# L3_xattn's queries by halves of two token tiles, one batch each, in a perceiver kernel on Trainium2

## The chip, the cores and the metric

The kernel runs on one core of a Trainium2 chip. A core has TensorE (PE, matrix products; the loading of its stationary operand is a row of its own, PEld), VectorE (DVE), ScalarE (ACT), GpSimd (POOL) and SyncE (SP), which issues the DMAs. Each engine works through its own queue in order and waits on semaphores of the others. The metric is the device time of one launch in microseconds; a figure for a kernel is the median of its runs. Lines of a profile name a line of the kernel's source (L702), an engine, an operation and the tiles it writes and reads.

## The reference: what is computed

The program is a perceiver of four layers. x holds 2 batches of 256 latent tokens with 256 features, the context 2 batches of 4096 tokens. Each layer adds a cross-attention to the context, a self-attention and a feed-forward block to x. The change touches only the cross-attention of the last layer, L3_xattn, and in it only the way of the queries:

```python
def _focus(x, focusing_factor):
    x = jnp.abs(jnp.where(x >= 0, x, LEAKY_SLOPE * x)) + EPS
    nrm = x.mean(axis=-1, keepdims=True)
    return jax.nn.softmax(jnp.log(x) * focusing_factor, axis=-1) * nrm
...
q = _focus(q @ Wq.T, focusing_factor)
k = _focus(k @ Wk.T, focusing_factor)
qh, kh, vh = (_to_heads(q), _to_heads(k), _to_heads(v))
qh = _topk_sparsify(qh)      # of each head's 16 features the 11 largest stay, the rest become 0
kh = _topk_sparsify(kh)
k_mean = kh.mean(axis=1)
z_inv = jnp.einsum('bnd,bd->bn', qh, k_mean) + EPS
kv = jnp.einsum('bnc,bnd->bcd', kh / sqrt_l, vh / sqrt_l)
y = jnp.einsum('bnc,bcd->bnd', qh, kv) / z_inv[..., None]
...
return y @ Wp.T
```

Here n is the 256 latent tokens for the queries, and x is layer-normalized ahead of the block.

## The kernel before

The 512 latent tokens (T) of both batches stand as four tiles of 128 tokens (NT = 4), two to a batch. x is kept with features on the partitions, as two chunks of 128 features. The blocks run one after the other. The context's keys for L3 are sharpened, ranked and summed much earlier, in the shadow of the cross-attentions of layers 0 and 1 (class `Focus`, called from the two attentions' step loop); these use `Focus.weigh` with four tiles and `Focus.sparsify`, which ranks on VectorE. L3_xattn itself (`l3_xattn`) has only the queries left:

1. `net.center` and `net.measure` take the mean off x and find each token's reciprocal deviation (`rstd`). The kept sums of keys (`focus.kc`) are turned and multiplied by `wv` to one small matrix for each batch (`kv_ps`, then the tiles `kv`).
2. For each token tile TensorE multiplies x by `wq` into a quarter of `q_ps`, a PSUM tile of two banks. `Focus.magnitudes` (L620, L621) reads it twice on ScalarE, as the positive and the scaled negative part, each with its sum over features, and POOL adds the two parts.
3. `Focus.weigh` takes the logarithm of all four tiles in one ScalarE instruction (L628), the product with the focusing factor on POOL (L632), the negative maximum of each token on VectorE (L634) and one exponential for each tile on ScalarE (L637). [...]
4. `sparsify_by_products` finds each feature's rank in its head. POOL scales the result (L687). The features are laid out so that feature e of all eight heads of a chunk stand side by side; then 15 comparisons on VectorE (`ge`, L699), shifted by 1 to 15 features, cover all pairs. Each is added to and taken from the rank by products with the identity (L702) and its negative (L703), which accumulate in PSUM. A comparison covers all four tiles; the rank has two banks with two tiles each, so each comparison is followed by four products. At the end VectorE keeps what has a rank below 11 (L706), one instruction for each bank, into `kept`.
5. Then, tile by tile, TensorE turns `kept` (`from_tokens`, L582, copied out by L219 as `qT`), multiplies it by the batch's matrix (`lin_ps`), VectorE forms the reciprocal and the quotient `y` (L1916 to L1920), TensorE turns `y` and a copy brings it to `yT`. `add_projection` multiplies by `wp` and adds x.

PSUM has three kinds of buffers here: two `mm` banks (also those of `from_tokens`), two `sc` tiles of two banks each (`q_ps` and `rank`) and two `acc` banks (`lin_ps`). The order of the instructions in each engine's queue in this block is not written by hand: the framework's scheduler arranges the instructions from their order in the program and from its own estimates. The next block, L3_attn, begins with POOL fills of its tiles, which wait until the tiles of L3_xattn are free.

Of the kernel before, what the change touches and what calls it, by code (L numbers as in the profile page):

```python
# [19 lines left out]
F32 = mybir.dt.float32  # L20
BF16 = mybir.dt.bfloat16
I32 = mybir.dt.int32
AF = mybir.ActivationFunctionType
ALU = mybir.AluOpType
AX = mybir.AxisListType

P = 128
NB = 2
S = 256
# [564 lines left out]
class Focus:  # L594
# [28 lines left out]
    def weigh(self, y, total, factor):  # L623


        nc = self.nc
        top, norm = (self.net.sm(NT, name=n, tag=n) for n in ("f_top", "f_norm"))
# [8 lines left out]
        for t in range(NT):  # L636
            nc.scalar.activation(  # L637
                y[:, t, :], y[:, t, :], AF.Exp, bias=top[:, t : t + 1], accum_out=norm[:, t : t + 1]
            )
            if t % 2:  # L640
                yield
# [39 lines left out]
    def sparsify_by_products(self, pool, out, y, factor):  # L681

        nc, net = self.nc, self.net
        N8, G = NT * ND, H // ND
        w = y.rearrange("p t (m e) -> p (t m) e", m=ND)
        for t in range(NT):
            nc.gpsimd.tensor_scalar(out[:, t, :], y[:, t, :], factor[:, t : t + 1], 1.0, ALU.mult, ALU.mult)  # L687
        minus = pool.tile([P, P], BF16, name="minus", tag="minus", bufs=1)
        nc.vector.tensor_scalar_mul(minus, net.ident16, -1.0)
        rank = net.sc("rank").rearrange("p i (h e) -> p i h e", e=P)  # L690
        half = N8 // 2
        for i in range(2):
            nc.tensor.matmul(
                rank[:, i], lhsT=net.ident16, rhs=self.rank0.unsqueeze(1).to_broadcast([P, half, P]), start=True, stop=False
            )
        for s in range(1, DH):
            n = (DH - s) * G
            ge = pool.tile([P, N8, P], BF16, tag="ge", name="ge", bufs=3)
            nc.vector.tensor_tensor(ge[:, :, :n], w[:, :, :n], w[:, :, P - n :], ALU.is_ge)  # L699
            for i in range(2):  # L700
                of = ge[:, i * half : (i + 1) * half, :n]
                nc.tensor.matmul(rank[:, i, :, P - n :], lhsT=net.ident16, rhs=of, start=False, stop=False)  # L702
                nc.tensor.matmul(rank[:, i, :, :n], lhsT=minus, rhs=of, start=False, stop=s == DH - 1)  # L703
        flat = out.rearrange("p t d -> p (t d)").rearrange("p (i h e) -> p i h e", i=2, e=P)
        for i in range(2):
            nc.vector.scalar_tensor_tensor(flat[:, i], rank[:, i], float(KEEP), flat[:, i], ALU.is_lt, ALU.mult)  # L706
# [1156 lines left out]
def l3_xattn(net, x):  # L1863
# [4 lines left out]
    with tc.tile_pool(name="l3x", bufs=1, reuse_waits="tile") as big, tc.tile_pool(name="l3x_w", bufs=2, reuse_waits="tile") as work:  # L1868
# [27 lines left out]
        total = net.sm(2, NT, name="f_total", tag="f_total")  # L1896
        q_ps = net.sc("q_ps").rearrange("p i (t d) -> p (i t) d", d=D)
        for t in range(NT):
            at = slice(t * P, (t + 1) * P)
            net.matmuls(q_ps[:, t, :], [(c[:, at], wq[:, d, :]) for d, c in enumerate(norm.chunks)])  # L1900
            focus.magnitudes(work, q, total, t, q_ps[:, t, :], (norm.rstd[:, t : t + 1], low[:, t : t + 1]))
        factor = net.sm(NT, name="f_factor", tag="f_factor")
        run(focus.weigh(q, total, factor))
        kept = big.tile([P, NT, D], F32, name="kept", tag="kept")
        focus.sparsify_by_products(work, kept, q, factor)
        yT = big.tile([P, ND, T], F32, name="yT", tag="yT")
        G = H // ND
        for t in range(NT):
            at, b = slice(t * P, (t + 1) * P), t * P // S
            qT = work.tile([P, ND, P], F32, name="qT", tag="qT")  # L1910
            net.from_tokens(lambda m, k: qT[:, m : m + k, :], kept[:, t, :], ND)
            ps = net.acc("lin_ps")[:, : ND * (P + G)].rearrange("p (m e) -> p m e", m=ND)
            for m in range(ND):
                net.matmuls(ps[:, m, :], [(qT[:, m, :], weigh[b, m])])
            r = net.sm(ND, G, name="r")
            nc.vector.tensor_scalar_add(r, ps[:, :, P:], 1e-6)  # L1916
            nc.vector.reciprocal(r, r)
            y = work.tile([P, D], F32, name="y", tag="y")
            for m in range(ND):
# [408 lines left out]
```

## Time and profile before

| what | value |
|---|---|
| median of 3 runs | 2512.33 us |
| lowest and highest run | 2512.18 and 2951.45 us |
| the profiled execution's own time | 2515.34 us |
| its span, first to last instruction | 2513.4 us |
| mean granted TensorE clock in it | 0.958 |
| first `low` of L3_xattn's queries (L620) starts at | 2098.93 us |
| first comparison (L699) starts at | 2114.53 us |
| first transpose of `kept` (L582) starts at | 2125.83 us |
| projection of L3_xattn starts at | 2140.07 us |

Times within the profile are counted from the start of the span. The granted clock is a share of TensorE's full speed. A line of the timeline gives start, length, engine, source line, operation, result and operands with their shapes, how many instructions were merged, and in square brackets how long the engine was idle before and who ended that. The length of an instruction contains its own run-through time, so two neighbours on an engine can overlap in such lines.

### The profile page before, as it was taken

What the parts mean: (1) busy time and instruction counts of PE and PEld (TensorE: products, weight loads), DVE (VectorE), ACT (ScalarE), POOL (GpSimd) and SP (SyncE); (2) the same over time, 40 slices, a digit from 0 to 9 for tenths busy, and PEclk for the clock granted to TensorE, in tenths of its full rate; (3) what the DMA queues carried; (4) which work ended last, traced back from release to release, by engine and by line L of the source; (5) the groups of instructions that cost most, each with busy time, mean ns of one, the idle gap of its engine ahead of it and who ended that gap; (6) DMA issues with size and microseconds to landing.
All of it is one profiled execution on the core that took longest, in us unless ns stands there. A gap on an engine that the chain in (4) does not pass through costs nothing.

```text
span 2513.4 us, 42846 instructions
## 1 busy us (share of the span) xinstructions
PE 2336.0 (93%) x17142; PEld 1252.9 (50%) x17142; DVE 1549.4 (62%) x2719; ACT 1093.2 (43%) x1917; POOL 333.2 (13%) x505
## 2 busy tenths in 40 slices
PE   7999999999999689999999999989999996889998
PEld 3455455544544364554454544554448453455454
DVE  4878888788736757877878778443241354334343
ACT  2456555555615333555555565531131252123232
POOL 3000001000024602000010000000011031002120
PEclk9999999999989799999999999989999997798989
DMA  5432232132010133322222220201232100100100
GB/s 185 138 105 86 88 96 94 52 111 64 10 38 35 48 103 108 101 91 90 90 94 86 77 98 28 83 14 43 96 100 93 43 18 14 34 21 12 58 12 21
DMA packets 97798, 174.42 MB, mean 69 GB/s; under 512 B 15120, under 2 KB 63888, under 8 KB 96704
## 3 DMA queue, kind: packets, MB, share of 16 engines
q1 hardware_dynamic: 97600, 171.68, 21.1%
q8 instruction: 136, 2.23, 0.4%
q14 instruction: 62, 0.51, 0.1%
HBM read 154.25 MB, written 0.59 MB: 62 GB/s over the span
## 4 chain that ended last, share of the span: by engine, by line
PE 57%; DVE 6%; ACT 2%; issue 1%; POOL 0%; DMA 0%; SPq 0%; ACTq 0%; DVEq 0%; POOLq 0%
PE s L1113 6%; PE s L1137 5%; PE proj L180 5%; PE attn_acc L1161 5%; PE v_ps L180 4%; PE expert L180 2%; PE k_ps L1034 2%; PE s L180 2%; PE c_acc L1753 2%; PE s L1430 2%; PE ffn_ps L180 2%; DVE mx L1121 2%; PE scores L342 1%; PE f_ps L180 1%; PE kc_sum L180 1%; PE qk_ps L180 1%
## 5 line engine op out<-in xcount | busy, mean ns | idle before, releaser
L1121 DVE TENSOR_REDUCE mx<-s 128x2 f32<-128x1024 f32 x512 | 603.2, 1221 | 224.6 <-PE s L1113 221.8
L1147 ACT ACTIVATE p<-s 128x1024 f32<-128x1024 f32 x512 | 496.0, 1021 | 255.8 <-PE s L1137 253.8
L1137 PE MATMUL s<-xa_q,xa_k 32*128 32x256 f32 x4096 | 342.3, 403 | 26.0 <-DVE mx L1121 23.0
L1113 PE MATMUL s<-xa_k,xa_q 32*128 32x512 f32 x2048 | 338.7, 642 | 7.0 <-ACT p L1147 2.3
L1137 PEld LDWEIGHTS s<-xa_q,xa_k 32*128 32x128 f32 x4096 | 212.7, 184 | 167.5 <-issue 92.6
L1161 PE MATMUL attn_acc<-p,xv 128*32 128x256 f32 x4096 | 276.2, 386 | 0.7 <-ACT p L1147 0.7
L1113 PEld LDWEIGHTS s<-xa_k,xa_q 32*128 32x128 f32 x2048 | 111.4, 183 | 124.7 <-issue 60.6
L667 DVE TENSOR_TENSOR ge<-fy 128x960 bf16<-128x960 f32 (+14 forms) x240 | 169.5, 706 | 6.5
L1161 PEld LDWEIGHTS attn_acc<-p,xv 128*32 128x32 f32 x4096 | 107.4, 109 | 131.4 <-issue 84.4
L621 POOL TENSOR_TENSOR fy<-fy,low 128x256 f32<-128x256 f32 x64 | 46.4, 725 | 881.3 <-ACT fy L620 881.1
L669 DVE TENSOR_TENSOR rank<-rank,ge 128x960 bf16<-128x960 bf16 (+14 forms) x240 | 104.2, 434 | 6.0
L671 DVE TENSOR_TENSOR rank<-rank,ge 128x960 bf16<-128x960 bf16 (+14 forms) x240 | 100.8, 420 | 2.6
L387 POOL TENSOR_SCALAR p<-p,r 128x128 f32<-128x128 f32 (+1 forms) x192 | 82.6, 442 | 127.0 <-DVE r L383 72.4
L1081 ACT COPY xv<-v_ps 128x512 f32<-128x512 f32 x64 | 37.6, 587 | 135.7 <-PE v_ps L180 135.7
L368 ACT ACTIVATE p<-p,top 128x256 f32<-128x256 f32 (+1 forms) x128 | 57.1, 447 | 66.6 <-DVE top L356 65.3
L180 PE MATMUL f_ps<-f_wk,f_ctx 128*128 128x256 f32 x256 | 68.9, 400 | 0.6 <-DMA f_ctx<-in_ctxT 0.6
L1034 PE MATMUL k_ps<-ctx_k,w_L0x_wq 128*64 128x512 f32 x256 | 66.0, 612 | 3.2 <-DMA ctx_k<-in_ctxT 2.9
L180 PE MATMUL v_ps<-w_L0x_wv,ctx_v 128*128 128x256 f32 x256 | 65.6, 400 | 0.8 <-ACT k_dense L1047 0.8
L180 PEld LDWEIGHTS f_ps<-f_wk,f_ctx 128*128 128x128 f32 x256 | 44.4, 189 | 43.3 <-issue 26.5
L1753 PE MATMUL c_acc<-pT,ctx_n 128*128 128x256 f32 x256 | 62.0, 387 | 4.2 <-ACT pT L1726 3.0
L180 PE MATMUL kc_sum<-f_tok,fy 128*128 128x257 f32 x256 | 64.2, 393 | 0.0
L180 PE MATMUL v_ps<-w_L1x_wv,ctx_v 128*128 128x256 f32 x256 | 63.8, 392 | 0.0
(478 smaller groups left out, 3366.8 us busy)
## 6 DMA issues: line engine op xcount, KB each, us to landing
ctx_k<-in_ctxT SPq DMA_DIRECT2D x128, 512.0 KB
ctx_v<-in_ctxT SPq DMA_DIRECT2D x64, 256.0 KB
xa_k<-k_dense SPq DMA_DIRECT2D x512, 32.0 KB
f_ctx<-in_ctxT SPq DMA_DIRECT2D x32, 256.0 KB
f_tok<-in_ctx SPq DMA_DIRECT2D x16, 512.0 KB
ctxT<-in_ctxT SPq DMA_DIRECT2D x16, 512.0 KB
ctx_n<-in_ctx SPq DMA_DIRECT2D x16, 512.0 KB
xa_k<-key_masks SPq DMA_DIRECT2D x128, 8.0 KB
```

The lines of the kernel that those rows point to most:

```text
L180: self.nc.tensor.matmul(out, lhsT=lhsT, rhs=rhs, start=i == 0, stop=i == len(pairs) - 1)
L387: nc.gpsimd.tensor_scalar(p[:, j, :nk], p[:, j, :nk], r[:, j : j + 1], 1.0, ALU.mult, ALU.mult)
L667: nc.vector.tensor_tensor(ge[:, :, :n], w[:, :, :n], w[:, :, P - n :], ALU.is_ge)
L669: nc.vector.tensor_tensor(rank[:, :, P - n :], rank[:, :, P - n :], ge[:, :, :n], ALU.add)
L671: nc.vector.tensor_tensor(rank[:, :, :n], rank[:, :, :n], ge[:, :, :n], ALU.subtract)
L1034: nc.tensor.matmul(ps[i * HR : (i + 1) * HR, :], lhsT=self.wk[:, d, c * HR : (c + 1) * HR], rhs=ctx[:, d, :], start=d == 0, stop=d == ND - 1,)
L1113: nc.tensor.matmul(pairs[i // 2][:, i % 2, :], lhsT=self.q[u][rows, qt * P : (qt + 1) * P], rhs=k[rows, :], start=True, stop=True,)
L1121: nc.vector.tensor_reduce(mx[:, qt, 2 * i : 2 * i + 2, kc], sc, AX.X, ALU.max)
L1137: nc.tensor.matmul(pairs[i // 2][:, i % 2, kk * S : (kk + 1) * S], lhsT=k[rows, at], rhs=self.q[u][rows, :], start=True, stop=True,)
L1147: nc.scalar.activation(p, sc, AF.Exp, scale=DH**-0.5)
L1161: nc.tensor.matmul(self.acc[i * HP : (i + 1) * HP, :S], lhsT=v[:, 2 * k2 + kk, at : at + HP], rhs=ps[i // 2][:, i % 2, kk * S : (kk + 1) * S],
L1753: nc.tensor.matmul(accs[m], lhsT=of[:, (k + i) % (KC // P), m * P : (m + 1) * P], rhs=pT[:, i, :], start=k + i == 0, stop=k + i == KT - 1,)
```

## The change

`weigh` and `sparsify_by_products` take the number of tiles from what they are given, or work on two tiles. In `l3_xattn` the queries are split by batch. A half's `q_ps` is now one `mm` bank, and each half has its own sums and factors. All products and magnitudes of both halves come first in the program, then `weigh` of the one and of the other half, then for each half ranking and right behind it turning and weighing of its two tiles. Each half's comparison covers two tiles, is followed by two products and accumulates in its own bank of `rank`. There are four `ge` buffers of half the size instead of three. The negative identity `minus` is made once, ahead of the halves.

```diff
--- before.py
+++ after.py
@@ -623,8 +623,8 @@
     def weigh(self, y, total, factor):
 
 
-        nc = self.nc
-        top, norm = (self.net.sm(NT, name=n, tag=n) for n in ("f_top", "f_norm"))
+        nc, n = self.nc, y.shape[1]
+        top, norm = (self.net.sm(n, name=name, tag=f"{name}{n}") for name in ("f_top", "f_norm"))
         nc.scalar.activation(y, y, AF.Ln, bias=self.eps)
 
         ready = self.net.sm(1, name="ready", tag="ready")
@@ -633,7 +633,7 @@
         yield
         nc.vector.tensor_reduce(top, y, AX.X, ALU.max, negate=True)
         yield
-        for t in range(NT):
+        for t in range(n):
             nc.scalar.activation(
                 y[:, t, :], y[:, t, :], AF.Exp, bias=top[:, t : t + 1], accum_out=norm[:, t : t + 1]
             )
@@ -678,32 +678,26 @@
             nc.gpsimd.tensor_scalar(y[:, t, :], y[:, t, :], factor[:, t : t + 1], 1.0, ALU.mult, ALU.mult)
         yield
 
-    def sparsify_by_products(self, pool, out, y, factor):
+    def sparsify_by_products(self, pool, out, y, factor, rank):
+
 
         nc, net = self.nc, self.net
-        N8, G = NT * ND, H // ND
+        n4, G = 2 * ND, H // ND
         w = y.rearrange("p t (m e) -> p (t m) e", m=ND)
-        for t in range(NT):
+        for t in range(2):
             nc.gpsimd.tensor_scalar(out[:, t, :], y[:, t, :], factor[:, t : t + 1], 1.0, ALU.mult, ALU.mult)
-        minus = pool.tile([P, P], BF16, name="minus", tag="minus", bufs=1)
-        nc.vector.tensor_scalar_mul(minus, net.ident16, -1.0)
-        rank = net.sc("rank").rearrange("p i (h e) -> p i h e", e=P)
-        half = N8 // 2
-        for i in range(2):
-            nc.tensor.matmul(
-                rank[:, i], lhsT=net.ident16, rhs=self.rank0.unsqueeze(1).to_broadcast([P, half, P]), start=True, stop=False
-            )
+        rank = rank.rearrange("p (h e) -> p h e", e=P)
+        nc.tensor.matmul(
+            rank, lhsT=net.ident16, rhs=self.rank0.unsqueeze(1).to_broadcast([P, n4, P]), start=True, stop=False
+        )
         for s in range(1, DH):
             n = (DH - s) * G
-            ge = pool.tile([P, N8, P], BF16, tag="ge", name="ge", bufs=3)
+            ge = pool.tile([P, n4, P], BF16, tag="ge", name="ge", bufs=4)
             nc.vector.tensor_tensor(ge[:, :, :n], w[:, :, :n], w[:, :, P - n :], ALU.is_ge)
-            for i in range(2):
-                of = ge[:, i * half : (i + 1) * half, :n]
-                nc.tensor.matmul(rank[:, i, :, P - n :], lhsT=net.ident16, rhs=of, start=False, stop=False)
-                nc.tensor.matmul(rank[:, i, :, :n], lhsT=minus, rhs=of, start=False, stop=s == DH - 1)
-        flat = out.rearrange("p t d -> p (t d)").rearrange("p (i h e) -> p i h e", i=2, e=P)
-        for i in range(2):
-            nc.vector.scalar_tensor_tensor(flat[:, i], rank[:, i], float(KEEP), flat[:, i], ALU.is_lt, ALU.mult)
+            nc.tensor.matmul(rank[:, :, P - n :], lhsT=net.ident16, rhs=ge[:, :, :n], start=False, stop=False)
+            nc.tensor.matmul(rank[:, :, :n], lhsT=self.minus, rhs=ge[:, :, :n], start=False, stop=s == DH - 1)
+        flat = out.rearrange("p t (m e) -> p (t m) e", m=ND)
+        nc.vector.scalar_tensor_tensor(flat, rank, float(KEEP), flat, ALU.is_lt, ALU.mult)
 
 
     def start(self, b, pool):
@@ -1893,37 +1887,49 @@
         q = big.tile([P, NT, D], F32, name="q", tag="q")
         low = big.tile([P, NT], F32, name="low_rstd", tag="low_rstd")
         nc.vector.tensor_scalar_mul(low, norm.rstd, -0.01)
-        total = net.sm(2, NT, name="f_total", tag="f_total")
-        q_ps = net.sc("q_ps").rearrange("p i (t d) -> p (i t) d", d=D)
-        for t in range(NT):
-            at = slice(t * P, (t + 1) * P)
-            net.matmuls(q_ps[:, t, :], [(c[:, at], wq[:, d, :]) for d, c in enumerate(norm.chunks)])
-            focus.magnitudes(work, q, total, t, q_ps[:, t, :], (norm.rstd[:, t : t + 1], low[:, t : t + 1]))
-        factor = net.sm(NT, name="f_factor", tag="f_factor")
-        run(focus.weigh(q, total, factor))
+        focus.minus = big.tile([P, P], BF16, name="minus", tag="minus")
+        nc.vector.tensor_scalar_mul(focus.minus, net.ident16, -1.0)
+
         kept = big.tile([P, NT, D], F32, name="kept", tag="kept")
-        focus.sparsify_by_products(work, kept, q, factor)
+        rank = net.sc("rank")
+        parts = []
+        for b in range(NB):
+            total = net.sm(2, 2, name="f_total", tag="f_total2")
+            factor = net.sm(2, name="f_factor", tag="f_factor2")
+            q_ps = net.mm("q_ps").rearrange("p (t d) -> p t d", d=D)
+            for i in range(2):
+                t = 2 * b + i
+                at = slice(t * P, (t + 1) * P)
+                net.matmuls(q_ps[:, i, :], [(c[:, at], wq[:, d, :]) for d, c in enumerate(norm.chunks)])
+                focus.magnitudes(
+                    work, q[:, 2 * b : 2 * b + 2], total, i, q_ps[:, i, :], (norm.rstd[:, t : t + 1], low[:, t : t + 1])
+                )
+            parts.append((q[:, 2 * b : 2 * b + 2], total, factor))
+        for part in parts:
+            run(focus.weigh(*part))
         yT = big.tile([P, ND, T], F32, name="yT", tag="yT")
         G = H // ND
-        for t in range(NT):
-            at, b = slice(t * P, (t + 1) * P), t * P // S
-            qT = work.tile([P, ND, P], F32, name="qT", tag="qT")
-            net.from_tokens(lambda m, k: qT[:, m : m + k, :], kept[:, t, :], ND)
-            ps = net.acc("lin_ps")[:, : ND * (P + G)].rearrange("p (m e) -> p m e", m=ND)
-            for m in range(ND):
-                net.matmuls(ps[:, m, :], [(qT[:, m, :], weigh[b, m])])
-            r = net.sm(ND, G, name="r")
-            nc.vector.tensor_scalar_add(r, ps[:, :, P:], 1e-6)
-            nc.vector.reciprocal(r, r)
-            y = work.tile([P, D], F32, name="y", tag="y")
-            for m in range(ND):
-                nc.vector.tensor_tensor(
-                    y[:, m * P : (m + 1) * P].rearrange("p (h e) -> p h e", e=DH),
-                    ps[:, m, :P].rearrange("p (h e) -> p h e", e=DH),
-                    r[:, m, :].unsqueeze(2).to_broadcast([P, G, DH]),
-                    ALU.mult,
-                )
-            net.from_tokens(lambda m, k: yT[:, m : m + k, at], y, ND)
+        for b, (y, _, factor) in enumerate(parts):
+            focus.sparsify_by_products(work, kept[:, 2 * b : 2 * b + 2], y, factor, rank[:, b])
+            for t in range(2 * b, 2 * b + 2):
+                at = slice(t * P, (t + 1) * P)
+                qT = work.tile([P, ND, P], F32, name="qT", tag="qT")
+                net.from_tokens(lambda m, k: qT[:, m : m + k, :], kept[:, t, :], ND)
+                ps = net.acc("lin_ps")[:, : ND * (P + G)].rearrange("p (m e) -> p m e", m=ND)
+                for m in range(ND):
+                    net.matmuls(ps[:, m, :], [(qT[:, m, :], weigh[b, m])])
+                r = net.sm(ND, G, name="r")
+                nc.vector.tensor_scalar_add(r, ps[:, :, P:], 1e-6)
+                nc.vector.reciprocal(r, r)
+                y = work.tile([P, D], F32, name="y", tag="y")
+                for m in range(ND):
+                    nc.vector.tensor_tensor(
+                        y[:, m * P : (m + 1) * P].rearrange("p (h e) -> p h e", e=DH),
+                        ps[:, m, :P].rearrange("p (h e) -> p h e", e=DH),
+                        r[:, m, :].unsqueeze(2).to_broadcast([P, G, DH]),
+                        ALU.mult,
+                    )
+                net.from_tokens(lambda m, k: yT[:, m : m + k, at], y, ND)
         return net.add_projection(x, wp, [yT[:, d, :] for d in range(ND)])
 
 
```

## The prediction

> **What bounds the kernel now.** I read the head of the page first: TensorE is busy for 93% of the span, so only a stretch in which it waits can give time back.
>
> ```profile
> span 2513.4 us, 42846 instructions
> PE 2336.0 (93%) x17142; PEld 1252.9 (50%) x17142; DVE 1549.4 (62%) x2719; ACT 1093.2 (43%) x1917; POOL 333.2 (13%) x505
> ```
>
> Then I cut the stretch the change touches into stages: magnitudes, logarithm to exponent, ranking, turning and weighing. They lie between 2098.9 us, when the first `low` starts, and 2140.07 us, when the last projection starts. That is 41.2 us, 1.6% of the span, so no outcome reaches a 2% change. The stage table (columns: stretch, length, then each engine's busy time and count, granted TensorE clock, DMA):
>
> ```profile
> 2098.90:2107.40 8.50, 4.48 (x17) 2.69 (x16) 0.48 (x2) 4.09 (x17) 2.17 (x3) 0.86 0.00 0
> 2107.40:2114.50 7.10, 0.00 (x0) 0.00 (x0) 2.04 (x4) 5.78 (x11) 1.84 (x2) 0.50 0.00 0
> 2114.50:2125.10 10.60, 8.99 (x60) 5.29 (x59) 10.03 (x18) 0.00 (x0) 6.36 (x4) 0.81 0.01 2
> 2125.10:2140.10 15.00, 8.59 (x33) 5.81 (x33) 6.21 (x21) 1.86 (x5) 0.00 (x0) 0.63 0.00 0
> ```
>
> In each stage one engine works and the others wait: ScalarE from logarithm to exponent, VectorE in the ranking (10.03 of 10.60 us), nobody in the turning, which is a relay. The timeline shows the relay's hand-overs:
>
> ```profile
> 2107.39 1.28 ACT L628 ACT_TABLE_LOAD   x1
> ...
> 2108.68 1.15 ACT L628 ACTIVATE q<-q,eps 128x1024 f32<-128x1024 f32 x1
> 2109.85 1.28 ACT L637 ACT_TABLE_LOAD   x1
> 2109.93 1.12 POOL L632 TENSOR_SCALAR q<-q,vectors 128x1024 f32<-128x1024 f32 x1 [1.76 <-ACT q L628]
> 2111.08 1.22 DVE L634 TENSOR_REDUCE f_top<-q 128x4 f32<-128x1024 f32 x1 [2.88 <-POOL q L632]
> ...
> 2114.53 1.13 DVE L699 TENSOR_TENSOR ge<-q 128x960 bf16<-128x960 f32 x1
> ...
> 2115.93 6.36 POOL L687 TENSOR_SCALAR kept<-q,f_factor 128x256 f32<-128x256 f32 x4 [4.88 <-DVE f_factor L645]
> ...
> 2125.08 1.29 DVE L706 SCALAR_TENSOR_TENSOR kept<-rank,kept 128x512 f32<-128x512 f32 x2 [0.41 <-PE rank L703]
> ```
>
> Nothing is turned before 2125.8, when all comparisons are over. The change lets the second half's ranking lie beside the first half's turning.
>
> **Part 1, magnitudes to exponent.** As built, TensorE's queue puts all eight query products behind the second batch's `kv_ps`, which ended at 2099.41. Two products (0.60 us each) and a rank start (0.38) that stood ahead of it are gone, so it ends near 2099.0. The first product then takes 1.13 (the row of the second tile's `q_ps`) and `low` starts at 2100.15 instead of 2098.93: 1.2 us lost. From there:
> - One tile's two activations take 1.02 us (2098.93 to 2099.95). Before, each tile waited for a product of 1.13 that itself waited for the last tile's activation, a period of 2.25 to 2.9. Now the halves have a bank each: tile 0, the wait of 1.20, tile 1, and tile 2 at once: 2100.15 + 1.02 + 1.20 + 1.02 + 1.02 = 2104.4.
> - The queue as built loads the logarithm's table here (1.28), takes the first half's logarithm (0.63, the row of a 128x512 square), tile 3's activations (1.02), waits for POOL's sum (0.8), takes the second logarithm (0.63) and loads the exponent's table (1.28): 2110.1. No table is loaded twice, since both logarithms precede both exponents.
> - POOL's power product (0.56, half of 1.12) and VectorE's maximum (0.68 for half) of the first half lie beside tile 3 and the second logarithm. They would cost 1.3 us uncovered.
> - Two exponents (half of 2.08): 2111.1, then a reciprocal. The first comparison starts at 2111.25, not 2114.53: 3.3 us gained.
>
> **Part 2, the first half's ranking.** Each of 15 comparisons halves. From the eleven last comparisons (5.77 us for 4224 elements) VectorE does 0.96 elements per ns plus 0.06 us each. A half has 3840 elements: 4.0 + 15 x 0.06 = 4.9 us. The scale factors' small operations add 0.25. The four POOL products come on top: three comparisons (768, 576 and 448 elements) were about 0.27 longer than their neighbours. [...] I take 6.25: 2117.5. POOL's own four products (6.36 us before) start near 2112.4 and the first two are done 3.2 us later, under cover of the comparisons. The next half's first comparison (0.56) fills the wait for the last rank sum, then `kept` of one half takes 0.69: 2118.8. TensorE starts cold: the first eight rank products took 2.95 us at clock 0.51. Its first four comparisons then need 2.9 us where VectorE needs 2.0, and four `ge` buffers cover this lag.
>
> **Part 3, the second half with the first half's turning in its midst.** VectorE has 14 comparisons (3360 elements: 3.5 + 0.85) and for tiles 0 and 1 two times 0.19 + 0.26 + 0.49 (rows of `r` and `y`): 6.25 us. Added waits: VectorE's `r` waits for `lin_ps` with comparisons queued behind it; TensorE's `lin_ps` waits for the copy `qT`, and its transposes of `y` wait for VectorE, with rank products queued behind. Walking both queues in their built order with these durations puts 0.5 us of waits on top, so the second `kept` (0.69) ends at 2126.2 if TensorE is at full clock. At half clock, rank start and products (8192 columns at 1.2 per ns: 6.8), two `lin_ps` at 1.27 and four transposed pairs (about 2) make 11.4 us, and `kept` ends at 2130.9.
>
> Which clock? The rows that bear on it are these, cut from 2118.65:
>
> ```profile
> 2118.65:2122.00 3.35, 3.22 (x21) 1.95 (x20) 3.19 (x6) 0.00 (x0) 3.35 (x3) 1.00 0.00 0
> 2122.00:2125.10 3.10, 2.84 (x34) 2.22 (x31) 2.69 (x9) 0.00 (x0) 0.29 (x1) 1.00 0.03 5
> 2125.10:2128.50 3.40, 1.24 (x7) 0.83 (x7) 2.19 (x6) 0.37 (x1) 0.00 (x0) 1.00 0.00 0
> 2128.50:2132.00 3.50, 2.27 (x10) 1.65 (x11) 1.34 (x5) 0.37 (x1) 0.00 (x0) 0.55 0.00 0
> ```
>
> After 3.4 us with TensorE 36% busy, the clock fell to half, though no gap there was longer than a microsecond. [...] By the row, the thin last comparisons and that gap are just such a lightly used window, and it starts cold for about 3.4 us and then, fully loaded, warms again: 1.7 us later. I take the row: 2127.9.
>
> **Part 4, the end.** Two tiles instead of four follow the last `kept`. Before, the transposes of the first to fourth tile started at 2125.83, 2128.57, 2131.91 and 2135.55, and the projection at 2140.07. One such step and the end cost 2.74 + 4.52 = 7.3 us warm and 3.64 + 4.52 = 8.2 cold. I take 7.7: the projection starts at 2135.6, 4.5 us earlier. What follows (projection, POOL's fills, L3_attn) is unchanged and shifts whole; its clock phase may give or take 1 us. Edits I cost at nothing: the `minus` tile moved to a longer-lived pool (still made once, at 2091.5, beside TensorE's mean), the renamed small tiles, and one more dummy exponent of one column per partition, which the built ScalarE queue carries in L1_xattn (at most 0.3 us there). SP's queue and its DMAs are the same.
>
> The profiled execution took 2515.34 us (span 2513.4 plus 1.9 around it); less 4.5 this is 2510.8. The median of the runs is 2512.33, so I forecast 2507.8.
>
> **Rivals.**
> - *Overlap at full clock.* The gap is too short to cool TensorE: 2126.2 + 7.3 = 2133.5, a gain of 6.6, 2505.7. For it: the clock held through 2125.1 to 2128.5. Against: it fell right after.
> - *Half clock throughout.* 2130.9 + 8.2 = 2139.1: a gain of 1, 2511.3. For it: the clock stayed at half from 2128.5 to the projection. Against: the ranking itself warmed it in 2.95 us.
> - *Slower: the two relays queue up instead of overlapping.* If each `lin_ps`, `r`, `y` and transpose stops the ranking for its whole chain, the second half costs two turning steps (2 x 3.64) plus cold ranking (6.8) plus `kept` (0.7). From 2118.8 this gives 2133.6, and with the end of 8.2, 2141.8: 1.7 us later, 2514.0. It decides if less than 1.7 us of those 14 overlap. Against: the queues as built put five to seven rank products between a tile's steps.
> - *The change doesn't take hold*: halves that share a tile's waits would stay in sequence and only pay 15 x 0.06 + 1.2: 2514.4. The separate banks and waits as built speak against it.
>
> **How the numbers follow.** Forecast (gain 3 to 6) 45%; full clock (6 to 8) 22%; half clock (0 to 3) 18%; the two slower ones 15%. The range from 2504.5 to 2512.0 leaves out the slower cases and the gains above 7.8. All of these lie far within 2%, about what a measurement of this kernel can tell from no change: within 98.5%, faster 0.5%, slower 1%.
>
> **What would show it.** Right: the first `low` near 2100.2 and the first half-size `ge` near 2111.3, the first transposes of `kept` some 7 us earlier than at 2125.83, `lin_ps` rows among the rank rows, and a stretch from first `low` to projection of about 35 us. Wrong: comparisons that wait for rank products by more than 1 us in the second half (clock), VectorE idle before `r` for over a microsecond per tile (relay), or a second pair of table loads. It would also be wrong if stretches far from this one moved by microseconds.

## The result, and the profile after

The changed kernel takes 2506.42 us (median of 20 runs), the kernel before 2520.47 (20 runs beside them). The ratio is 0.9949, with a 95% interval of 0.9932 to 0.9966: 12.9 us faster (8.6 to 17.1), and within the 2% that count as no change here. The ratio leaves out a slow run of the kernel before (2951.45 us), so the 12.9 us are not the difference of the two medians. The median of 2512.33 that the forecast started from was that of three runs; over twenty, the kernel before stands 8 us higher.

The head of the page hardly moves:

```profile
span 2511.1 us, 42873 instructions
PE 2330.6 (93%) x17142; PEld 1251.9 (50%) x17142; DVE 1554.9 (62%) x2737; ACT 1094.5 (44%) x1921; POOL 331.8 (13%) x506
```

The stretch shows more. All stages start at other times in every profile, so from here on times within L3_xattn are counted from the block's first product, the `mean` that takes the average off x (at 2090.91 us in the profile before, at 2095.62 in the one after), up to the same product of L3_attn. This stretch took 54.84 us before and takes 47.72 now. The stage table of the changed kernel (columns as before: stretch, length, busy time and count of each engine, granted clock, DMA) has five rows: magnitudes, logarithm to exponent, the first half's ranking, the second half's ranking with the first half's turning, the end up to the projection:

```profile
2104.85:2109.05 4.20, 1.90 (x8) 1.02 (x6) 0.76 (x2) 2.96 (x13) 1.46 (x2) 1.00 0.00 0
2109.05:2116.05 7.00, 1.61 (x4) 0.98 (x5) 1.85 (x6) 6.12 (x13) 2.84 (x4) 0.54 0.00 0
2116.05:2122.70 6.65, 5.55 (x30) 3.02 (x29) 6.65 (x21) 0.86 (x4) 4.16 (x4) 0.72 0.00 0
2122.70:2130.35 7.65, 6.54 (x47) 4.50 (x47) 7.14 (x25) 1.21 (x4) 0.00 (x0) 1.00 0.01 2
2130.35:2137.45 7.10, 3.83 (x16) 2.44 (x16) 2.25 (x9) 1.30 (x4) 0.00 (x0) 0.72 0.00 0
```

The fourth row is what the change is about. Both engines work there at once, VectorE for 7.14 and TensorE for 6.54 of 7.65 us, and the clock is full. The timeline shows the overlap itself:

```profile
2122.68 0.68 DVE L700 SCALAR_TENSOR_TENSOR kept<-rank,kept 128x512 f32<-128x512 f32 x1
2123.28 2.02 DVE L696 TENSOR_TENSOR ge<-q 128x448 bf16<-128x448 f32 x4
...
2123.42 0.44 PE L582 MATMUL feat_ps<-ident,kept 128*128 128x128 f32 x2 [1.02 <-DVE kept L700]
...
2124.32 0.73 PE L180 MATMUL lin_ps<-kv,qT 128*128 128x136 f32 x4
...
2125.22 0.17 DVE L1922 TENSOR_SCALAR r<-lin_ps 128x16 f32<-128x16 f32 x1
...
2125.46 0.49 DVE L696 TENSOR_TENSOR ge<-q 128x320 bf16<-128x320 f32 x1
...
2129.66 0.68 DVE L700 SCALAR_TENSOR_TENSOR kept<-rank,kept 128x512 f32<-128x512 f32 x1
...
2134.10 1.27 PE L180 MATMUL lin_ps<-kv,qT 128*128 128x136 f32 x4 [0.32 <-ACT qT L219]
...
2137.47 5.09 PE L180 MATMUL proj<-yT,w_L3x_wq 128*128 128x512 f32 x8 [0.46 <-ACT yT L219]
```

Between `kept` of the first half and `kept` of the second VectorE goes back and forth between comparisons (L696) and quotients (L1922 to L1926) without a wait of half a microsecond. Only the last tile's `lin_ps` takes 1.27 us instead of 0.73: the clock has fallen by then (it falls at 2133.5 us).

Counted from the block's first product:

| event | before | after | after earlier by |
|---|---|---|---|
| first `low` | 8.02 | 9.23 | -1.2 |
| first comparison | 23.62 | 20.43 | 3.2 |
| first transposes of `kept` | 34.92 | 27.80 | 7.1 |
| last `kept` done | 35.46 | 34.72 | 0.7 |
| projection | 49.16 | 41.85 | 7.3 |
| L3_attn's first product | 54.84 | 47.72 | 7.1 |

So L3_xattn itself is 7.1 us shorter, and the runs show 12.9. L3_attn, whose instructions are the same, takes 101.88 us in this profile and took 104.48 before, another 2.6. Its two rows, before and after, differ in TensorE's busy time and in the granted clock, 0.89 and 0.93:

```profile
2145.75:2250.23 104.48, 88.86 (x716) 51.55 (x717) 39.62 (x69) 26.01 (x34) 4.88 (x13) 0.89 0.07 21
2143.34:2245.22 101.88, 84.87 (x717) 49.68 (x717) 39.61 (x69) 26.02 (x34) 4.89 (x13) 0.93 0.07 22
```

Where the rest is, and why an unchanged block should move, is part of the experiments.

### The profile page after: what moved, and what is told of

Its sections match the earlier page's. It is cut to its first block, busy times and chain, and to the rows that moved or that the text cites. A ratio compares the mean times of both kernels' runs of the same rounds, so it can differ in the third digit from the quotient of the medians.

```text
span 2511.1 us, 42873 instructions
## 1 busy us (share of the span) xinstructions
PE 2330.6 (93%) x17142; PEld 1251.9 (50%) x17142; DVE 1554.9 (62%) x2737; ACT 1094.5 (44%) x1921; POOL 331.8 (13%) x506
## 4 chain that ended last, share of the span: by engine, by line
PE 55%; DVE 6%; ACT 3%; issue 1%; POOL 1%; DMA 0%; ACTq 0%; SPq 0%; DVEq 0%; POOLq 0%
PE s L1107 6%; PE s L1131 5%; PE proj L180 5%; PE attn_acc L1155 5%; PE v_ps L180 4%; PE expert L180 2%; PE k_ps L1028 2%; PE s L180 2%; PE c_acc L1747 2%; PE s L1424 2%; PE ffn_ps L180 2%; DVE mx L1115 2%; PE f_ps L180 1%; PE kc_sum L180 1%; PE kq_ps L180 1%
```

## The experiments

Ratios are to the kernel before on the same chip; where none is given, a kernel ran once, with a profile. The lengths come from that profile: L3_xattn and L3_attn from first product to first product, and from the first product of L3_xattn to the end of the span.

| kernel | median us, runs | ratio (95%) | L3_xattn | L3_attn | L3_xattn to the end |
|---|---|---|---|---|---|
| before | 2520.47, 20 | 1 | 54.84 | 104.48 | 422.5 |
| before, again | 2521.45, 14 | 1.0006 (0.9983 to 1.0029) | 56.58 | 106.18 | 428.9 |
| after | 2506.42, 20 | 0.9949 (0.9932 to 0.9966) | 47.72 | 101.88 | 415.5 |
| after, again | 2504.92, 22 | 0.9946 (0.9933 to 0.9959) | 48.10 | 101.94 | 416.0 |
| tile places alone | 2516.80, 14 | 0.9994 (0.9983 to 1.0006) | 54.84 | 104.48 | 425.5 |
| part 1 alone | 2512.94, 20 | 0.9984 (0.9969 to 0.9999) | 54.19 | 105.72 | 426.0 |
| parts 2 to 4 alone | 2511.92, 20 | 0.9979 (0.9966 to 0.9992) | 50.52 | 106.11 | 422.7 |
| turning last | 2515.02, 12 | 0.9988 (0.9969 to 1.0007) | 54.27 | 105.83 | 426.1 |
| a gap between the halves | 2508.95, 1 | | 54.64 | 104.49 | 425.4 |
| scaling on ScalarE | 2512.38, 1 | | 47.86 | 105.69 | 419.5 |
| early table | 2502.63, 1 | | 47.70 | 101.94 | 415.8 |
| keys' matrix later | 2512.89, 1 | | 46.72 | 102.75 | 415.5 |
| those three together | 2508.03, 13 | 0.9965 (0.9952 to 0.9978) | 47.32 | 106.17 | 419.6 |
| TensorE kept busy | 2504.73, 6 | 0.9948 (0.9930 to 0.9966) | 45.06 | 104.89 | 415.9 |

**The changed kernel again**, without an edit.

> The changed kernel once more, timed against the kernel before. Theory: the change gives back about 7 us, all of it in L3_xattn, whose stretch from its own mean product to that of L3_attn took 54.84 us before and 47.72 us after; that stretch should again take 47.5 to 48.0 us, and the ratio should lie near 0.997. Rival: something outside L3_xattn gains as well (the earlier ratio of 0.9949 is some 13 us); then the ratio stays near 0.995 and the unchanged stretches are shorter again.

The gain repeats (ratio 0.9946), and so do the two blocks: 48.10 and 101.94. Neither was a chance of one execution. The ratio is the one that the rival named, not 0.997, and L3_attn, outside L3_xattn, is shorter again too.

**Tile places alone.** The halves bring four more small tiles, so that what is allocated behind them moves. Before, with only those tiles, each filled once:

```diff
+        for name, shape in (("f_total", (2, 2)), ("f_factor", (2,)), ("f_top", (2,)), ("f_norm", (2,))):
+            nc.gpsimd.memset(net.sm(*shape, name=name, tag=f"{name}2"), 0.0)
```

> The kernel before with nothing of the change but its four further small tiles in the pool of small tiles (so that all later tiles lie where the changed kernel has them), each only filled once by GpSimd. Theory (only the stretch L3_xattn changes): ratio 1.000 within 0.002, the stretch from mean product to mean product 54.6 to 55.1 us. Rival (the tiles' places shift the time of the context attentions): ratio near 0.998 or below.

No change (0.9994), and both blocks as before to a hundredth. So the gain doesn't come from the places of the tiles.

**One part at a time.** Part 1 alone keeps the magnitudes and `weigh` by halves, and ranks and turns as before; parts 2 to 4 alone keep ranking and turning by halves behind the old magnitudes. Against the changed kernel:

```diff
# part 1 alone
-            ge = pool.tile([P, n4, P], BF16, tag="ge", name="ge", bufs=4)
+            ge = pool.tile([P, N8, P], BF16, tag="ge", name="ge", bufs=3)
...
+        focus.sparsify_by_products(work, kept, q, factors)
-        for b, (y, _, factor) in enumerate(parts):
+        for t in range(NT):
# parts 2 to 4 alone
+        run(focus.weigh(q, total, factor))
-        for part in parts:
-            run(focus.weigh(*part))
```

> Part 1 alone: products, magnitudes, logarithms and exponents by halves, the ranking and turning as before. Theory: the first comparison comes 3.2 us earlier after the mean product (20.4 instead of 23.6 us), and all of it is kept: stretch 51.6 us. Rival (the early half only pays with a ranking by halves): the first comparison waits for the second half's exponents, 1.0 us is lost again, 52.6 us; or nothing is gained, 54.8.

> Parts 2 to 4 alone: products to exponents as before, then ranking and turning by halves. Theory: of the 7.1 us that L3_xattn gained, 3.2 were there at the first comparison, so this keeps 3.9: stretch 50.9 us. Rival (the clock): with the longer pause of TensorE ahead of the ranking its second half is cold, 1.7 to 4.5 us later: 52.6 to 55.4 us.

Part 1 alone brings 0.65 us of the stretch, not the 3.2 that it brings to the first comparison. A comparison over four tiles waits for four exponents, so the first one is only 2.2 earlier (21.42). The ranking takes 0.5 longer (12.3 from the first comparison to the last `kept`, 11.8 before); VectorE once waits 0.37 us for rank products. The turning takes 0.4 longer and the projection with what follows 0.65; the clock falls at 34.5 us instead of 37.9. Parts 2 to 4 alone bring 4.3: the first comparison needs the exponents of two tiles only and comes 1.6 us earlier, the projection gains another 4.0 with the overlap, and 1.3 are lost behind the projection, which runs mostly at half clock. The two parts alone sum to 5.0, together they give 7.1.

**Turning last.** The halves are ranked as in the changed kernel, but turned only after both:

```diff
-        flat = out.rearrange("p t (m e) -> p (t m) e", m=ND)
-        nc.vector.scalar_tensor_tensor(flat, rank, float(KEEP), flat, ALU.is_lt, ALU.mult)
...
+        flat = kept.rearrange("p t d -> p (t d)")
+        nc.vector.scalar_tensor_tensor(flat, rank.rearrange("p i f -> p (i f)"), float(KEEP), flat, ALU.is_lt, ALU.mult)
+        for b in range(NB):
```

> The changed kernel, but what is kept is decided in one instruction for both halves after all comparisons, so that nothing can be turned beside the ranking. Theory (the gain of the second part is overlap): the two first turning steps come back, about 2 x 3 us, less the 0.7 us and the gap of about 1 us that fall away between the halves: stretch 52 to 53 us. Rival (halves rank faster by themselves): 47.7 to 49 us.

Without the overlap the stretch takes 54.27 us, more than expected. The first comparison is as early as in the changed kernel (20.42), the last `kept` ends at 33.18 instead of 35.46 before, and then the turning gives 0.9 back and the projection and the rest 0.8; here the clock falls at 34.8 us. So 6.5 of the 7.1 us hang on the turning amid the second half's ranking.

**A gap between the halves.** Four more passes over `kept` in the first half (estimated at 0.69 us each, 2.8 in all), with a bound of 1000 that every rank meets, so that they change nothing:

```diff
+        for _ in range(4 if first else 0):
+            nc.vector.scalar_tensor_tensor(flat, rank, 1000.0, flat, ALU.is_lt, ALU.mult)
         nc.vector.scalar_tensor_tensor(flat, rank, float(KEEP), flat, ALU.is_lt, ALU.mult)
```

> The changed kernel with four further passes of VectorE over the first half's kept values (they multiply by one), so that TensorE idles for about 5 us between the halves. [...] By the row I took (a lightly used window is enough) the changed kernel should have been cold already, so nothing but the 2.8 us is added: 50.5 us.

The stretch takes 54.64 us, 6.9 more than in the changed kernel. The first half's `kept` is done 4.1 us later (the passes were expected to take 2.8), the second half's 6.9. The clock fell, as these rows show (stretches of 3.4 us; the first number after the length is TensorE's busy time, the last but two the granted clock):

```profile
2106.00:2109.40 3.40, 2.53 (x23) 1.70 (x20) 3.40 (x11) 0.00 (x0) 1.95 (x3) 0.99 0.00 0
2109.40:2112.80 3.40, 0.00 (x0) 0.00 (x0) 3.40 (x7) 0.00 (x0) 0.00 (x0) 1.00 0.00 0
2112.80:2116.20 3.40, 2.32 (x9) 1.70 (x10) 0.90 (x2) 0.37 (x1) 0.00 (x0) 0.51 0.02 5
```

Behind this gap, which fills a whole stretch of 3.4 us, the clock was 0.51; behind the one of the changed kernel, 1.02 us, it stayed at 1.00. But this doesn't tell whether the length of the gap decides or, as in the reading of the row, a lightly used window, since a stretch of 3.4 us with nothing in it is both.

**The kernel before again.** The gain in the runs was still larger than what the two blocks gave.

> The kernel before, unchanged, measured against itself. Open is that the changed kernel gained some 13 us in the runs, while the two stretches read from the profiles, L3_xattn (54.84 to 47.72 us) and L3_attn (104.48 to 101.88), give 9.7. Theory A (profiles of before are repeatable in these two stretches, and the comparison has no bias): ratio 1.000 within 0.0015, L3_xattn 54.8, L3_attn 104.5, and the feed-forward block after it near 96.6 us instead of the 93.74 of the first profile, which would be a chance of that one execution. Rival B (the comparison itself leans to one side by what every measured kernel but one shows, 3 to 4 us): ratio near 0.9985, below 0.9995. Rival C (before has more than one form of L3_xattn or L3_attn, and the first profile showed the rarer one): L3_xattn or L3_attn differs from the above by over 1 us.

Measured against itself the kernel before gives 1.0006, so no lean of the comparison is seen; its interval, 0.9983 to 1.0029, still has room for one of 4 us. And this profile of the same program shows L3_xattn at 56.58 and L3_attn at 106.18 us, 1.7 each above the first one. Everything up to the fourth tile's transposes agrees within 0.2 us. Then come these rows of the first profile before:

```profile
2125.43:2128.84 3.41, 1.58 (x10) 1.17 (x10) 1.86 (x6) 0.37 (x1) 0.00 (x0) 1.00 0.00 0
...
2139.08:2142.49 3.41, 2.95 (x5) 1.33 (x6) 0.00 (x0) 0.37 (x1) 0.00 (x0) 0.50 0.00 0
2142.49:2145.91 3.42, 2.64 (x7) 0.93 (x6) 1.37 (x2) 0.00 (x0) 0.73 (x1) 1.00 0.00 0
```

and these of the second, cut at the same distances from the block's first product (2098.36 us there):

```profile
2132.83:2136.24 3.41, 1.47 (x9) 1.06 (x10) 1.96 (x6) 0.37 (x1) 0.00 (x0) 1.00 0.00 0
...
2146.48:2149.89 3.41, 2.88 (x5) 1.49 (x6) 0.12 (x1) 0.37 (x1) 0.00 (x0) 0.50 0.00 0
2149.89:2153.31 3.42, 3.42 (x5) 1.35 (x4) 0.69 (x1) 0.00 (x0) 0.00 (x0) 0.50 0.00 0
```

The projection started 49.16 us after the first product in the one and 49.31 in the other. In the one TensorE was busy for 2.95 us of the stretch ahead of 51.6, and the clock rose there; in the other for 2.88, and it rose one stretch of 3.4 us later. That the start 0.15 us later decided over the 1.7 us is argued from these two profiles; busy time alone doesn't explain it, since in the second profile's own ranking the clock rose behind 2.77.

This is why the stretches are cut as they are. In all fourteen traces, from L3_xattn into L3_attn, the clock changes only at points that lie a multiple of 3.4 us apart: in the first profile of before at 2105.0, 2118.6, 2128.9, 2142.5, 2166.4, 2169.8 and 2180.1 us, differences of 4, 3, 4, 7, 1 and 3 times 3.41. The grid doesn't start with the span: counted back in such steps, its first border lies between 0 and 3.1 us behind the start, differently in each trace. On this block, though, the borders lie nearly alike: in every trace one lies 13.9 to 14.6 us behind the block's first product. So by then the program has fallen into step with the grid; what does this stays open.

In the ranking and the turning, for stretches that begin 13 to 45 us behind that product, TensorE's busy time in the stretch between two borders sorts what follows without an exception. Of the stretches at full clock in all fourteen traces, 17 were busy for 2.09 us of 3.41 or less, and behind each the clock fell; 41 were busy for 2.26 or more, and behind each it held. At half clock, 53 with 2.40 or less stayed there, and behind 23 with 2.77 or more it rose. (The expectation below names 2.08 and 2.34, from fewer borders.) The longest gap doesn't sort them: behind a stretch of part 1 alone without a gap above 0.85 us the clock fell, behind six in other kernels with a gap of 1.02 it held. Twelve of the 17 stretches behind which it fell had no gap above 1 us. The bounds are read off the same traces that they sort, and just ahead of the 13 us they fail: the clock held behind 2.0 us (parts 2 to 4 alone) and stayed at half behind 2.80 (keys' matrix later).

**TensorE kept busy.** The sorting can be tested ahead of a run. In the changed kernel the stretch from 2130.0 to 2133.4 us was busy for 1.65 us, and the clock fell there. Six products that nobody needs are put where TensorE waits for a copy or for VectorE:

```diff
+        spare = net.sc("spare")
+
+        def fill(of, n):
+            for _ in range(n):
+                net.matmuls(spare[:, 0, :D], [(net.ident, of)])
...
                 net.from_tokens(lambda m, k: qT[:, m : m + k, :], kept[:, t, :], ND)
+                fill(kept[:, t, :], 1 if b else 0)
...
                     net.matmuls(ps[:, m, :], [(qT[:, m, :], weigh[b, m])])
+                fill(qT.rearrange("p m e -> p (m e)"), 2 if b else 0)
```

> The changed kernel with six more products in the turning of the last two tiles (kept or qT times the identity into a bank nobody reads), each placed where TensorE waits for a copy or for VectorE. In all traces so far the granted clock changes only at points that lie a multiple of 3.4 us apart, and at full clock it falls behind a 3.4 us stretch that was busy for 2.08 us or less (1.65 in the changed kernel, 37.8 us after the block's mean product) and holds behind one of 2.34 or more. Theory W (the busy share of such a stretch decides): the stretch that was busy 1.65 us is now busy 2.4 to 3.0, the clock stays full, the last tile's lin_ps takes 0.73 instead of 1.27, the projection 3.4 to 4.2 instead of 5.09, and L3_xattn 45.0 to 46.0 us instead of 47.7 to 48.1. Rival G (only the longest gap counts, or these products are not counted as activity): the clock falls at the same point, the added products run at half clock in the relay's way, and L3_xattn takes 48.0 to 49.0. L3_attn may take anything from 101.9 to 106.2 by its clock; with 101.9 and W the time is 2 us below the changed kernel (ratio 0.994), with 106.2 it is 2 us above (0.996).

L3_xattn takes 45.06 us, 2.7 less than in the changed kernel. These are the stretches in the changed kernel

```profile
2119.80:2123.20 3.40, 2.48 (x22) 1.70 (x20) 3.40 (x11) 0.00 (x0) 1.30 (x2) 1.00 0.00 0
2123.20:2126.60 3.40, 3.18 (x20) 2.08 (x21) 3.32 (x11) 0.37 (x1) 0.00 (x0) 1.00 0.02 5
2126.60:2130.00 3.40, 3.23 (x29) 2.41 (x27) 2.98 (x15) 0.65 (x2) 0.00 (x0) 1.00 0.00 0
2130.00:2133.40 3.40, 1.65 (x10) 1.11 (x10) 1.25 (x5) 0.74 (x2) 0.00 (x0) 1.00 0.00 0
2133.40:2136.80 3.40, 2.11 (x9) 1.32 (x7) 1.34 (x5) 0.37 (x1) 0.00 (x0) 0.51 0.00 0
```

and with the added products (cut at that trace's own borders, 0.4 us later)

```profile
2124.18:2127.59 3.41, 3.24 (x18) 2.49 (x18) 0.95 (x5) 0.69 (x3) 0.00 (x0) 1.00 0.00 0
2127.59:2131.01 3.42, 2.26 (x12) 1.56 (x12) 1.34 (x5) 0.66 (x2) 0.00 (x0) 1.00 0.00 0
2131.01:2134.42 3.41, 3.41 (x9) 1.50 (x10) 0.69 (x1) 0.00 (x0) 0.00 (x0) 1.00 0.00 0
```

TensorE is busy for 3.24 us in place of 1.65, and the clock holds. The added products also shorten the longest gap of that stretch, from 0.97 us to 0.09, so it is the comparison above, not this run, that tells busy time from gaps. The last `lin_ps` and the projection show what this gives:

```profile
2128.27 0.73 PE L180 MATMUL lin_ps<-kv,qT 128*128 128x136 f32 x4 [0.58 <-DVE qT L219]
2128.84 1.03 PE L180 MATMUL spare<-qT,ident 128*128 128x256 f32 x4
...
2130.87 3.70 PE L180 MATMUL proj<-yT,w_L3x_wq 128*128 128x512 f32 x8 [0.46 <-ACT yT L219]
```

0.73 for 1.27 and 3.70 for 5.09. But L3_attn then took 104.89 us and not 101.88, so that from L3_xattn to the end both kernels are level (415.9 and 415.5), and so are the runs (0.9948 and 0.9949).

**Three more attempts at the time ahead of the ranking.** The four products with the factors on ScalarE instead of POOL; the logarithm's table loaded early by a logarithm of one column per partition, with ScalarE's order written by hand and without the dummy exponents; the block of the keys' matrix (`kv_ps`) behind the magnitudes in the program; and all three at once.

```diff
# scaling on ScalarE
-            nc.gpsimd.tensor_scalar(out[:, t, :], y[:, t, :], factor[:, t : t + 1], 1.0, ALU.mult, ALU.mult)
+            nc.scalar.mul(out[:, t, :], y[:, t, :], factor[:, t : t + 1])
# early table
+        with tc.manual_schedule(engines={mybir.EngineType.Activation}):
+            nc.scalar.activation(net.sm(1, name="early", tag="early"), norm.rstd[:, 0:1], AF.Ln, bias=focus.eps)
```

> The changed kernel with the scaling by the factor on ScalarE instead of GpSimd. Theory (VectorE's comparisons and GpSimd's products lock each other out): the first half's 15 comparisons lose up to 1.1 us, the stretch from the first comparison to the first kept value goes from 6.63 to about 5.7 us, and L3_xattn from 47.7 to about 46.9 us. Rival (TensorE's cold start holds the comparisons through the four buffers): no change, 47.7 us.

> The changed kernel with the logarithm's table loaded by a one-column logarithm ahead of the first magnitude, where ScalarE waits for the query product, and ScalarE's order as written (four magnitudes, two logarithms, four exponents). Theory: ScalarE's chain bounds this part, so the second logarithm ends 0.7 us earlier after the mean product (17.2 instead of 17.9 us) and the stretch takes 47.0 us. Rival: GpSimd's sum and product set the second logarithm, nothing is gained, 47.7 us.

> The changed kernel with the turning and multiplying of the keys' sums moved behind the queries' magnitudes in the program, so that TensorE makes the query products first. Theory (my Part 1: the queries' products wait behind the keys' products): the first magnitude starts 1.5 us earlier after the mean product (7.7 instead of 9.2 us), and the stretch takes 46.2 us. Rival: the keys' copies then stand in ScalarE's and VectorE's queues between logarithm and comparisons and take the gain back, 47.7 us.

> The changed kernel with four more edits: the scaling by the factor on ScalarE instead of GpSimd, the logarithm's table loaded ahead of the first magnitude, the keys' products behind the queries' products, and ScalarE's order of magnitudes and weighing as written (no dummy exponents). Theory: 0.8 us from the lock between VectorE and GpSimd, 0.7 from the table and 1.5 from the earlier products: the stretch takes 44.7 us instead of 47.7. Rival (the relays behind them wait elsewhere): 46.5 to 48 us.

None brought what was hoped for. This is VectorE's line of the first half's later comparisons in the changed kernel, and below it are those with the scaling on ScalarE:

```profile
2118.05 4.72 DVE L696 TENSOR_TENSOR ge<-q 128x384 bf16<-128x384 f32 x13
...
2113.35 1.79 DVE L696 TENSOR_TENSOR ge<-q 128x384 bf16<-128x384 f32 x4
2115.32 0.42 DVE L696 TENSOR_TENSOR ge<-q 128x256 bf16<-128x256 f32 x1 [0.18 <-PE rank L698]
2115.91 2.17 DVE L696 TENSOR_TENSOR ge<-q 128x224 bf16<-128x224 f32 x8 [0.16 <-PE rank L698]
```

Both sets include the second half's first comparison. These 13 are busy for 4.38 us where the changed kernel has 4.72, 0.34 more with POOL's products beside them; but 0.34 of waits for TensorE, at half clock, took its place. The table load that was moved ahead had been hidden beside the last tile's product, since ScalarE waits for it either way (in the changed kernel's trace one load of 1.28 us stands ahead of the first logarithm and one ahead of the first exponential):

```profile
2100.23 0.47 ACT L620 ACTIVATE low<-q_ps,low_rstd 128x256 f32<-128x256 f32 x1 [1.68 <-PE q_ps L180]
```

The first comparison came only 0.25 us earlier. With the keys' matrix later the first `low` is 2.2 us earlier (7.04), the first comparison 0.15: the second logarithm stood behind a copy for the keys' matrix in ScalarE's queue, and VectorE's maximum of the second half stood ahead of the first comparison. The 1.0 us that its L3_xattn is shorter lies behind the projection (5.0 us to L3_attn's first product instead of 5.9). The three together had their first comparison 0.9 later. Their L3_xattn is 0.4 us shorter than the changed kernel's, but L3_attn takes 106.17, and the runs are slower (0.9965, beside the changed kernel's 0.9946; the intervals just touch).

## Why the prediction was right, and where it was wrong

The mechanism is the one forecast: the second half's ranking lies beside the first half's turning, and 6.5 of the 7.1 us in the block hang on that. That the time fell into the range, close to the 2507.8 forecast, is luck. The base was 8 us too low (2512.33 for 2520.47) and the gain 8 us too small (4.5 for 12.9), and the two cancel; the forecast gain from the base of twenty runs gives 2516.0, outside the range. By its steps:

- **Part 1, magnitudes to exponent: right.** The first `low` is 1.2 us later and the first comparison 3.2 earlier (forecast: 1.2 and 3.3). That no table is loaded twice held too.
- **Part 2, the first ranking: right in its sum.** From first comparison to `kept` done 7.3 us (forecast 7.55). The composition was off: the 6.25 us of the first half's comparisons contain 1.1 us of waits, by a lock between VectorE and POOL that no run shows. What the rows show is less. Before, three comparisons beside POOL's products took 0.18 to 0.20 us more than the mean of their neighbours, not 0.27. In the changed kernel three beside them took 0.68, 0.61 and 0.54 us, the same widths in the second half, without POOL, 0.49, 0.41 and 0.35; POOL's products of 128x256 took 0.86 to 1.20 us there, those of 128x512 ahead of the comparisons 0.69. By the run with the scaling on ScalarE the 13 later comparisons were busy for 0.34 less, and taking POOL away shortened the half by only 0.2, since TensorE at half clock came up behind. That "four `ge` buffers cover this lag" didn't hold in that run.
- **Part 3, the second half: here a step failed.** "By the row, the thin last comparisons and that gap are just such a lightly used window, and it starts cold." The gap meant is TensorE's between the halves, 1.02 us in the trace. The half did not start cold. From the first `kept` to the second 7.0 us passed, where the warm working gave 7.4 and the cold one 9.1. The full-clock rival, by which this gap is too short to cool TensorE, had the clock right here; the length of the gap would not have given the fall at 2133.5 us, behind a stretch without a gap above 0.97. The row had been read rightly as well: behind a stretch busy for 1.58 of 3.4 us (1.24 in the prediction's own cut) the clock fell before, and behind one of 1.65 it falls after. What failed was the claim that the new window is such a stretch. The stretch of 3.4 us that holds the thin last comparisons and 0.8 of the 1.0 us of gap is busy for 2.48 us, and the next one, with the transposes of `kept` and the second half's first products right behind the gap, for 3.18. The busy time was never added up for the forecast.
- **Part 4, the end: right** (7.1 for 7.7 us; from the first `low` to the projection 32.6 where about 35 were forecast). The relay of the last two tiles cooled TensorE after all, one tile before the projection. This is the light window that the step had looked for, in another place.
- **"What follows is unchanged and shifts whole; its clock phase may give or take 1 us": mis-sized.** L3_attn, with the same instructions in the same order, took from 101.88 to 106.18 us, and in the fourteen profiles this goes with its granted clock: 101.9 to 102.8 us in the four at 0.93, 104.5 to 104.9 and once 106.2 in the five at 0.89, 105.7 to 106.2 in the five at 0.87. With a gap in the block ahead of it, the changed kernel's L3_attn took 104.49, as in the first profile of before. The term is 4.3 us wide, not 2. The prediction named stretches that move by microseconds as a sign of being wrong, far from this one; the very next one did.
- **The base.** The sum was made against the profiled execution of 2515.34 us and the median of three runs. The second profile of before is 1.7 us longer in each of the two blocks, and 3.0 in the stretch behind L3_attn up to the next such product (96.7 us for 93.7, with 96.5 in the changed kernel, whose instructions there are the same): 428.9 us from L3_xattn to the end instead of 422.5. From 428.9 the changed kernel's 415.5 is a gain of 13.4, and the runs show 12.9. The other kernels with an interval agree: tile places 3.5 (runs 1.5), part 1 alone 2.9 (4.0), parts 2 to 4 alone 6.2 (5.3), turning last 2.8 (3.0), the three together 9.3 (8.8), TensorE kept busy 13.0 (13.1), each within its interval. So the 12.9 us may be 8.9 in L3_xattn and 4.3 in L3_attn, both against the longer form. That the longer form is the common one is argued from this agreement, not shown. Of the three profiles with this order of work (before twice, and tile places) two have the shorter blocks, and from the 425.5 of tile places only two kernels of seven leave their intervals, by 1 us or less. Ahead of L3_xattn the profiles differ by up to 16.5 us (its first product starts between 2081.85 and 2098.36), so they can't show whether anything changed there. What the runs gain beyond the 7.1 us stays open in its shares.

The full-clock rival came nearest within the block (6.6 forecast for the projection, 7.3 measured). The half-clock rival fell with the clock. The relay did not queue up: VectorE's longest wait for a `lin_ps` amid the ranking was 0.42 us.

## What to carry to other kernels

Work of two engines in turn is worth overlapping by halves even where each half's instructions get dearer: the 15 added comparisons were estimated at 0.9 us, against 6.5 that hang on the overlap. Before a forecast says of work like this that TensorE will be warm or cold, add up its busy time in the new order over stretches of 3.4 us; a gap of 1 us by itself said little here, a stretch that is half empty said much. And take more than one profile of the base: in a block that nobody touched the clock moved up to 4.3 us, and the block that was changed gained 7.1.

## What the hardware showed that was not expected

- The granted clock changed only on a grid of 3.4 us, which lay nearly alike on this block in all fourteen traces. In ranking and turning the busy share of one such stretch, not the longest gap in it, told whether the clock fell behind it: from full clock it fell behind all 17 with 2.09 us or less and behind none of the 41 with 2.26 or more.
- Elsewhere these bounds did not hold. About the block's last products, the full clock held behind stretches with 1.43 to 2.05 us and fell behind those with 1.41 or less, and in L3_attn stretches that the trace shows fully busy stayed at half clock, as in these rows of the first profile before. Busy time alone doesn't settle it there. Most products there are like those of the third line, with 32 rows (the 32 of 32*128) where the ranking's and the turning's have 128; whether that is why, no run tested:

```profile
2183.40:2186.80 3.40, 3.40 (x20) 1.95 (x18) 2.36 (x2) 0.00 (x0) 0.00 (x0) 0.50 0.00 0
...
2190.30:2193.70 3.40, 3.40 (x18) 1.98 (x20) 0.90 (x1) 0.71 (x1) 0.00 (x0) 0.50 0.00 0
...
2193.12 3.04 PE L1430 MATMUL s<-sa_q,sa_k 32*128 32x256 f32 x16
```

- With a projection that started 0.15 us later (49.31 for 49.16) the clock rose a whole stretch later, and L3_xattn took 1.7 us more. Six useless products gained 2.7 us in their block; the next block gave 3.0 back.
